# A macaron layer on one core: own phase plans for the first two and last two chunks, set-up in twelve steps, one more value and gate buffer

## The chip, the cores and the metric

The kernel runs on one core of a Trainium2 chip. The metric is the device time of one execution in microseconds (us). Three runs of the kernel before gave 1022.44, 1022.88 and 1028.41 us; the median is 1022.88 us.

## What is computed

The input x has 8 batches of 1024 positions with 256 channels. Three sublayers follow each other, each on a layer norm of its input:

```
x = x + 0.5 * ffn(layernorm(x))
x = x + attention(layernorm(x))
x = x + 0.5 * ffn(layernorm(x))
```

The feed-forward mixes each position with the one before it, and multiplies a sigmoid gate with a squared-ReLU network:

```
xr = mu_r * x + (1 - mu_r) * x_prev;  xk = mu_k * x + (1 - mu_k) * x_prev
ffn = sigmoid(xr @ W_r) * (square(relu(xk @ W_k)) @ W_v)
```

The attention has 16 heads of 16 channels. Each query looks at 40 fixed offsets back: 0 to 32, and 48, 64, 96, 128, 192, 256, 384. Its logit is `q.k * 0.25 * (1 + q.scale_embed[offset]) + pos_bias[offset]`; a softmax over the 40 logits weights the shifted values. The result is multiplied by a gain and by a sigmoid gate, and goes through an output projection.

## The kernel before

**Units of work.** A chunk is 256 positions; there are 32 (c = 0 to 31), four to a batch. A tile is 128 positions (tt = 0 to 63), two to a chunk. A pair is two chunks (i = 0 to 15). Each kind of work is a Python generator, whose `yield` cuts it into steps, and each step issues a few instructions:

- `f1`, `f2` (`ffn(c, "a")`, `ffn(c, "b")`): load of x (f1 only), statistics on DVE (L207), a chain of eight small POOL instructions for the normalisation (L212 to L219), normalised rows on ACT (L224) and their transposes on PE (L226), scaling on ACT (L241), the shifted part on DVE (L246), the products k, r and v on PE with relu, square and tanh on ACT (L263, L269, L271), the gated product on DVE (L278), the sum on POOL (L280), the output's DMA (L283, f2 only). f1 has 12 steps, f2 has 12.
- `p` (`project(c)`): statistics, normalisation and transposes as above, a split of the rows into two fp16 halves (L291, L292), the projections q, k, gate and value on PE (twelve fp16 matmuls each), `kst` on DVE (L317), `gt` on ACT (L329), the bias added to x on POOL (L341), `vn` on DVE (L343), and a DMA of the values to DRAM (L351).
- `far` (i, th) and `loc` (tt): the score products of far and near offsets on PE, copied out by ACT (L370) and written by DMA to DRAM (L397 and L411), from where a skewed read turns them into one row per query.
- `att` (`attend(tt)`), 18 steps: the skewed reads of the logits (`lg`, L425 and L429), reads of the shifted values (`vw`, `v3`, L435 to L445), the product `gp` with the scale embedding on PE, `lr` on DVE (L458), the bias on POOL (L461), maximum and subtraction on DVE (L464, L465), the exponential on ACT (L467) and, issued by ACT, the write of the probabilities to DRAM (L468), the far products on POOL (L482) and DVE (L489), the skewed read of the probabilities (`pd`, L497), the far sum on DVE (L505) and POOL (L508), eight transposes of pd on PE (L514) in two halves, each copied by ACT to `ptt` (L520), the value product `pv` on PE, division on DVE (L536 to L538), transposes (L547), the gate (L548), and for the chunk's second tile the output projection and the sum into x (L563). For a chunk's first tile the last step issues nothing.

All matmuls are issued by the helper `mm` (L195), so the profile gives them that line.

**The order.** There is no loop over chunks in which the work stands. Every step has a time: the place of its unit (c, tt/2 or 2i) plus an entry of the table `PLAN` for that kind and step, plus a shift of `WARP` for some kinds at chunks 0 to 3 and 22 to 31. All steps are sorted by these times and issued in this order, by hand (`tc.manual_schedule()`). The order counts per engine: each engine takes its instructions in the order in which they were issued, and waits for what the next one needs. DMAs of SP and ACT stand in their engines' queues in the same way. A unit of time is a chunk.

**Buffers.** `PVN = 5` buffers hold `vn` (read by the far products until two chunks later), `PGA = 4` hold the gate. Logits `lg` have four buffers, `pd` one, the transposes and pv share one PSUM bank, scores and gp have two banks for each half.

**Set-up** has three steps: the loads of weights; then zeros, and a scale, an fp16 cast and a remainder of the four attention weights as one block (L153 to L156); then the biases.

Of the kernel before, what the change touches and what calls it, by code (L numbers as in the profile page):

```python
# [12 lines left out]
ALU = mybir.AluOpType  # L13
# [6 lines left out]
NCH = B * N // 256  # L20
# [15 lines left out]
SF_T = 16 * ROW - 16  # L36
VPAD = 96
VROW = 2 * 8 * 17
PX1, PVN, PGA = 12, 5, 4
WS = 16.0  # L40
XN, LGB, PDB, PTB, YTB = 2, 4, 1, 2, 1

PLAN = {
    "setup": (94.301, 95.430, 96.861),
    "f1": (-6.891, -5.181, -4.113, -3.628, -3.556, -3.503, -3.223, -3.134, -3.030, -2.933, -2.814, -2.771),
    "p": (-2.636, -2.595, -2.382, -2.366, -2.209, -2.155, -2.084, -1.868, -1.644, -1.528, -1.432),
    "f2": (1.626, 1.748, 1.930, 2.004, 2.060, 2.208, 2.297, 2.414, 2.553, 2.580, 2.713, 4.437),
    "far": (  # L50
        (-0.987, -0.918),
        (-0.874, -0.608),
        (-0.990, -0.939),
        (-0.777, -0.772),
        (-0.751, -0.627),
        (-0.528, -0.523),
    ),
    "loc": (
        (-1.515, -1.348),
        (-0.848, -0.610),  # L60
        (-1.298, -1.048),
        (-1.496, -1.489),
    ),
    "att": (
        (-0.277, -0.025, -0.020, 0.011, 0.092, 0.296, 0.358, 0.413, 0.416, 0.471, 0.743, 0.779, 0.784, 0.838, 0.892, 0.971, 1.094, 13.222),
        (-0.404, 0.000, 0.016, 0.041, 0.111, 0.194, 0.295, 0.315, 0.427, 0.447, 0.621, 0.660, 0.673, 0.723, 0.824, 0.884, 0.938, 1.093),
    ),
}
WARP = {
    ("att", 0): 0.012, ("att", 1): 0.014, ("att", 2): 0.002, ("att", 3): -0.006, ("att", 22): 0.010, ("att", 23): 0.002, ("att", 24): -0.008, ("att", 25): 0.032, ("att", 26): 0.048, ("att", 27): 0.036, ("att", 28): 0.026, ("att", 29): -0.049, ("att", 30): -0.064, ("att", 31): -0.076,  # L70
    ("f1", 0): -1.203, ("f1", 1): -0.910, ("f1", 2): -0.739, ("f1", 3): 0.153, ("f1", 22): 0.006, ("f1", 23): 0.025, ("f1", 24): -0.009, ("f1", 25): -0.004, ("f1", 26): 0.009, ("f1", 27): 0.026, ("f1", 28): 0.017, ("f1", 29): 0.027, ("f1", 30): 0.045, ("f1", 31): 0.053,
    ("f2", 0): 0.006, ("f2", 1): 0.006, ("f2", 2): -0.013, ("f2", 3): 0.001, ("f2", 22): 0.006, ("f2", 23): -0.003, ("f2", 24): 0.043, ("f2", 25): 0.041, ("f2", 26): 0.025, ("f2", 27): 0.477, ("f2", 28): 0.422, ("f2", 29): 0.543, ("f2", 30): 0.373, ("f2", 31): 0.119,
    ("far", 0): -0.275, ("far", 2): -0.001, ("far", 22): 0.004, ("far", 24): 0.035, ("far", 26): 0.044, ("far", 28): 0.047, ("far", 30): -0.024,
    ("loc", 0): -0.699, ("loc", 1): -0.010, ("loc", 2): 0.023, ("loc", 3): 0.047, ("loc", 22): 0.037, ("loc", 23): 0.007, ("loc", 24): 0.043, ("loc", 25): 0.074, ("loc", 26): 0.045, ("loc", 27): 0.056, ("loc", 28): 0.007, ("loc", 29): 0.037, ("loc", 30): 0.014, ("loc", 31): 0.120,
    ("p", 0): -0.906, ("p", 1): -0.868, ("p", 2): -0.096, ("p", 3): 0.024, ("p", 22): -0.017, ("p", 23): -0.005, ("p", 24): 0.014, ("p", 25): 0.005, ("p", 26): -0.008, ("p", 27): -0.040, ("p", 28): 0.034, ("p", 29): 0.045, ("p", 30): 0.006, ("p", 31): -0.018,
}


# [5 lines left out]
def macaron(ctx: ExitStack, tc: tile.TileContext, x, wffn, watt, wo, cols, rows, pbias, se, mask, out):  # L84
    nc = tc.nc
# [14 lines left out]
    wa_hi = const.tile([128, 4, 2, 256], F16, name="wa_hi")  # L100
# [24 lines left out]
    def setup():  # L125
        with tc.tile_pool(name="setup", bufs=1) as sp:
            nc.sync.dma_start(w_f, wffn.rearrange("w (c p) d -> p w c d", p=128))
            wst = sp.tile([128, 4, 2, 256], F32, name="wst")
            nc.sync.dma_start(wst, watt.rearrange("w (c p) d -> p w c d", p=128))
            nc.sync.dma_start(row, rows.unsqueeze(0).to_broadcast([128, 2, 256]))  # L130
            zero = sp.tile([128, 4 * 512], F32, name="zero")
            nc.gpsimd.memset(zero, 0.0)
            nc.sync.dma_start(bias[:, 3].rearrange("p u e -> p (u e)"), pbias.to_broadcast([128, NO * 16]))
            msk = sp.tile([128, 3, NO], F32, name="msk")
            nc.sync.dma_start(msk, mask.rearrange("t p u -> p t u"))
            nc.sync.dma_start(wot, wo.rearrange("(c p) d -> p c d", p=128))
            se_f = sp.tile([128, NO], F32, name="se_f")
            nc.sync.dma_start(se_f, se.unsqueeze(0).to_broadcast([8, 16, NO]))
            yield
            nc.gpsimd.tensor_scalar(w_f[:, 2], w_f[:, 2], 0.25, 0.0, ALU.mult, ALU.add)  # L140
            for t in vw:
                nc.gpsimd.memset(t, 0.0)
            for t in ks:
                nc.gpsimd.memset(t[:, 0:LW], 0.0)
            for i in range(2):
                nc.sync.dma_start(v_d[i][0 : VPAD * VROW].rearrange("(p w) -> p w", p=VPAD), zero[:VPAD, :VROW])
            for sf in sf_d:
                nc.sync.dma_start(sf[0:PADF].rearrange("(p w) -> p w", p=16), zero[:16, : PADF // 16])
                for c0, c1, w in ((0, 5, 384), (5, 10, 384), (10, 15, 384), (15, 16, 368)):
                    o = PADF + c0 * ROW + ROW - 384  # L150
                    nc.sync.dma_start(flat(sf, o, (SF_T, 32), (ROW, c1 - c0), (1, w)), zero[:32, : (c1 - c0) * w])
            nc.sync.dma_start(flat(pd_d, NL * 16, (4 * SKEW, 128), (SKEW, 4), (1, SKEW - NL * 16)), zero[:, : 4 * 512])
            nc.vector.tensor_scalar(wst[:, 0], wst[:, 0], 0.25 * WS, None, ALU.mult)  # L153
            nc.vector.tensor_scalar(wst[:, 1:4], wst[:, 1:4], WS, None, ALU.mult)
            nc.scalar.copy(wa_hi, wst)
            nc.vector.tensor_tensor(wa_lo, wst, wa_hi, ALU.subtract)  # L156
            nc.vector.tensor_scalar(b_q, b_q, 0.25 * WS, None, ALU.mult)
            nc.vector.tensor_scalar(b_k, b_k, WS, None, ALU.mult)
            nc.vector.tensor_scalar(bv, bv, WS, None, ALU.mult)
            nc.vector.tensor_scalar(b_g, b_g, 0.5, None, ALU.mult)  # L160
            yield
            for t in range(3):
                nc.gpsimd.tensor_tensor(
                    bias[:, t], bias[:, 3], msk[:, t].unsqueeze(2).to_broadcast([128, NO, 16]), ALU.add
                )
            for c in range(2):
                nc.vector.tensor_scalar(wot[:, c], wot[:, c], gain[:, c : c + 1], 0.5 / WS, ALU.mult, ALU.mult)
            nc.vector.tensor_scalar(se_f, se_f, 4.0 / WS, None, ALU.mult)

            nc.vector.tensor_reduce(  # L170
                own.rearrange("p (h q) -> p h q", h=2),
                ident.rearrange("p (q h d) -> p h q d", q=4, h=2),
                AX.X,
                ALU.add,
            )
            nc.vector.tensor_reduce(
                kown.rearrange("p (h q) -> p h q", h=2),
                own.rearrange("p (h r q) -> p h q r", h=2, r=2),
                AX.X,
                ALU.add,  # L180
            )
            nc.vector.tensor_tensor(
                seb.rearrange("p u h q -> p u (h q)"),
                se_f.unsqueeze(2).to_broadcast([128, NO, 4]),
                kown.unsqueeze(1).to_broadcast([128, NO, 4]),
                ALU.mult,
            )
        lazy["pat"] = pool("pat", 2)
        lazy["pv1"] = pool("pv1", 2)
        yield  # L190
# [226 lines left out]
    def attend(tt):  # L417
# [149 lines left out]
    nc.vector.tensor_scalar(rest, col[:, 0:4], -1.0, 1.0, ALU.mult, ALU.add)  # L567
    steps = []
    move = lambda kind, place: place + WARP.get((kind, int(max(place, 0))), 0)
    add = lambda kind, place, gen, times: steps.extend(  # L570
        (move(kind, place) + t, kind, j, gen) for j, t in enumerate(times)
    )
    add("0", -100, setup(), PLAN["setup"])
    for c in range(NCH):
        add("f1", c, ffn(c, "a"), PLAN["f1"])
        add("p", c, project(c), PLAN["p"])
        add("f2", c, ffn(c, "b"), PLAN["f2"])
    for i in range(2 * B):
        for th in range(2 + 2 * (i % 2)):
            add("far", 2 * i, far(i, th), PLAN["far"][2 * (i % 2) + th])  # L580
    for tt in range(B * NT):
        add("loc", tt / 2, local(tt), PLAN["loc"][tt % 4])
        add("att", tt / 2, attend(tt), PLAN["att"][tt % 2])
    with tc.manual_schedule():
        for place, kind, j, gen in sorted(steps, key=lambda s: s[:3]):
            next(gen)
# [63 lines left out]
```

## Time and profile before

| | |
|---|---|
| median of three runs | 1022.88 us |
| the profiled execution: time, span | 1026.83 us, 1024.8 us |
| granted TensorE clock, mean | 0.971 |
| PE busy | 951.4 us (93%) |
| DVE, POOL, ACT busy | 831.9, 695.5, 610.4 us |
| DMA moved | 208.75 MB, 204 GB/s mean |

PE is TensorE's matmuls and PEld its weight loads, DVE the vector engine, ACT the scalar engine, POOL GpSimd, SP the engine that issues most DMAs. The ends of matmuls are modelled, so a busy PE is not one at its peak. A row such as "x<-y L224" is a group of instructions that write x from y at line 224. The chain that ended last is followed back from the last instruction; "issue" is time in which nothing shows that the engine waited for.

### The profile page before, as it was taken

What the parts mean: (1) busy time and instruction counts of PE and PEld (TensorE: products, weight loads), DVE (VectorE), ACT (ScalarE), POOL (GpSimd) and SP (SyncE); (2) the same over time, 40 slices, a digit from 0 to 9 for tenths busy, and PEclk for the clock granted to TensorE, in tenths of its full rate; (3) what the DMA queues carried; (4) which work ended last, traced back from release to release, by engine and by line L of the source; (5) the groups of instructions that cost most, each with busy time, mean ns of one, the idle gap of its engine ahead of it and who ended that gap; (6) DMA issues with size and microseconds to landing.
All of it is one profiled execution on the core that took longest, in us unless ns stands there. A gap on an engine that the chain in (4) does not pass through costs nothing.

```text
span 1024.8 us, 36078 instructions
## 1 busy us (share of the span) xinstructions
PE 951.4 (93%) x14592; PEld 781.3 (76%) x14592; DVE 831.9 (81%) x1670; ACT 610.4 (60%) x1218; POOL 695.5 (68%) x1240
## 2 busy tenths in 40 slices
PE   3888899999999999999999999999999999976775
PEld 2666688888888888888888888888888888854554
DVE  4446889988999789888999789988999789866761
ACT  3454666676666766676666766676666766543332
POOL 5434778767877688667787678767886778543641
PEclk9899999999999999999999999999999999988888
DMA  8257777768777776777877777688776777757530
GB/s 241 62 157 204 221 227 200 222 200 249 214 219 216 215 237 198 214 228 218 236 207 225 220 237 211 196 236 244 222 212 210 205 227 216 211 161 234 166 110 21
DMA packets 204365, 208.75 MB, mean 204 GB/s; under 512 B 77288, under 2 KB 162472, under 8 KB 204200
## 3 DMA queue, kind: packets, MB, share of 16 engines
q1 hardware_dynamic: 194984, 189.16, 64.8%
q10 hardware_dynamic: 9216, 17.31, 4.6%
q8 instruction: 114, 1.87, 0.8%
q14 instruction: 51, 0.42, 0.1%
HBM read 110.26 MB, written 96.14 MB: 201 GB/s over the span
## 4 chain that ended last, share of the span: by engine, by line
PE 81%; DMA 4%; POOL 4%; DVE 4%; issue 3%; ACT 2%; SPq 1%; ACTq 0%; POOLq 0%; DVEq 0%
PE p L195 55%; PE pv L195 6%; PE tra L195 5%; PE tra L514 5%; PE tr L226 5%; PE gp L195 4%; PE tra L547 1%; DMA lg<-sl 1%; ACT xn L224 1%; POOL y L213 1%; POOL x L280 1%; DMA sf<-sf 1%; DVE prod L505 1%; DMA pd<-pd 1%; DVE st L207 1%
## 5 line engine op out<-in xcount | busy, mean ns | idle before, releaser
L195 PE MATMUL p<-w_f,xm 128*128 128x256 f32 x1024 | 251.3, 389 | 0.0
L195 PEld LDWEIGHTS p<-w_f,xm 128*128 128x128 f32 x1024 | 187.5, 192 | 42.2 <-issue 12.7
L461 POOL TENSOR_TENSOR lg<-lg,bias 128x640 f32<-128x640 f32 x64 | 99.0, 1547 | 85.8 <-DVE lg L458 74.6
L195 PE MATMUL p<-xm,w_f 128*128 128x256 f32 x512 | 128.6, 396 | 8.4 <-DVE xm L248 5.2
L224 ACT ACTIVATE xn<-x,nb,y 128x256 f32<-128x256 f32 x192 | 104.9, 599 | 32.4 <-POOL nb L219 16.4
L241 ACT ACTIVATE xm<-tr,col 128x256 f32<-128x256 f32 x256 | 100.4, 475 | 39.8 <-PE tr L226 33.9
L195 PE MATMUL p<-kst,qst 64*32 64x256 f32 (+1 forms) x4096 | 123.6, 362 | 0.5 <-DVE kst L317 0.3
L246 DVE SCALAR_TENSOR_TENSOR xm<-tr,rest,xm 128x255 f32<-128x255 f32 x256 | 105.5, 474 | 21.2 <-ACT xm L241 19.9
L195 PEld LDWEIGHTS p<-xm,w_f 128*128 128x128 f32 x512 | 96.5, 198 | 25.6 <-issue 10.4
L508 POOL TENSOR_TENSOR far<-prod 128x272 f32<-128x272 f32 x64 | 49.0, 765 | 93.3 <-DVE prod L505 86.2
L280 POOL TENSOR_TENSOR x<-x,xm 128x512 f32<-128x512 f32 x64 | 81.9, 1279 | 39.9 <-DVE xm L278 39.9
L195 PE MATMUL p<-xh,wa_hi 128*128 128x256 f16 x384 | 105.1, 274 | 0.0
L195 PE MATMUL p<-xh,wa_lo 128*128 128x256 f16 x384 | 104.9, 273 | 0.0
L195 PE MATMUL p<-xl,wa_hi 128*128 128x256 f16 x384 | 104.9, 273 | 0.0
L482 POOL TENSOR_TENSOR prod<-vn,lg 128x272 f32<-128x272 f32 x144 | 94.9, 671 | 14.2 <-ACT lg L467 12.8
L520 ACT COPY ptt<-tra 128x512 f32<-128x512 f32 x128 | 74.7, 584 | 43.7 <-PE tra L514 27.8
L226 PE MATMUL tr<-ident,xn 128*128 128x128 f32 x384 | 66.4, 293 | 33.2 <-ACT xn L224 32.7
L505 DVE TENSOR_TENSOR prod<-prod 128x544 f32<-128x544 f32 (+2 forms) x120 | 93.6, 780 | 3.6
L195 PEld LDWEIGHTS pv<-vw,ptt 128*32 128x32 f32 x4096 | 69.2, 157 | 33.3 <-ACT ptt L520 17.3
L195 PEld LDWEIGHTS p<-kst,qst 64*32 64x32 f32 x4096 | 75.7, 122 | 22.9 <-issue 10.7
L317 DVE SCALAR_TENSOR_TENSOR kst<-p,col,kown 128x1024 f32<-128x1024 f32 x64 | 78.7, 1271 | 13.5 <-PE p L195 13.5
L514 PE MATMUL tra<-ident,pd 128*128 128x128 f32 x512 | 80.1, 280 | 10.3 <-DMA pd<-pd 6.7
(79 smaller groups left out, 2051.5 us busy)
## 6 DMA issues: line engine op xcount, KB each, us to landing
sl<-sl SPq DMA_DIRECT2D x256, 128.0 KB, 3.4
pd<-pd SPq DMA_DIRECT2D x64, 512.0 KB, 4.3
sf<-sf SPq DMA_DIRECT2D x184, 128.0 KB, 3.2
vw<-vd SPq DMA_DIRECT2D x128, 136.0 KB, 4.1
v<-vd SPq DMA_DIRECT2D x64, 272.0 KB, 4.4
lg<-sl SPq DMA_DIRECT2D x64, 264.0 KB, 3.9
pd<-lg ACTq DMA_DIRECT2D x64, 264.0 KB, 2.8
vd<-vn SPq DMA_DIRECT2D x32, 272.0 KB, 4.8
```

What stands on the lines that cost most here:

```text
L195: nc.tensor.matmul(o, l, r, start=start, stop=stop)
L224: nc.scalar.activation(xn, x2[:, i], AF.Identity, bias=nb[:, i : i + 1], scale=y[:, i : i + 1])
L226: nc.tensor.transpose(tr[:, c, i * 128 : i * 128 + 128], xn[:, c * 128 : c * 128 + 128], ident)
L241: nc.scalar.activation(xm[:, o, h], tr[:, h], AF.Identity, scale=mu[:, h : h + 1])
L246: nc.vector.scalar_tensor_tensor(x_[:, 1:256], tr[:, h, 0:255], m, x_[:, 1:256], ALU.mult, ALU.add)
L280: nc.gpsimd.tensor_tensor(x2, x2, xr, ALU.add)
L317: nc.vector.scalar_tensor_tensor(ks[g][:, o : o + 256], p[:, g].unsqueeze(2).to_broadcast([128, 256, 4]), b_k[:, g : g + 1], kown.unsqueez ...
L461: nc.gpsimd.tensor_tensor(la, la, bias[:, min(t, 3)].rearrange("p u e -> p (u e)"), ALU.add)
L482: nc.gpsimd.tensor_tensor(prod[:, k], shifted[k][1](), lf[:, k].unsqueeze(2).to_broadcast([128, 16, 17]), ALU.mult,)
L505: nc.vector.tensor_tensor(terms[:, 0:m], terms[:, 0:m], terms[:, n - m : n], ALU.add)
L514: nc.tensor.transpose(tr[:, pr * 128 : pr * 128 + 128], pd.rearrange("p (m e) -> p m e", e=8)[:, :, 4 * g + pr], ident,)
L520: nc.scalar.copy(ptt.rearrange("p q n -> p (q n)"), tr)
```

## The change

`PLAN` and `WARP` get new numbers throughout. Two further tables of the same form, `HEAD` and `TAIL`, give their own times to the units whose place is below 2 or at least 30. Set-up has twelve steps: loads; zeros; then for each of the four weights a scale with the cast, and the remainder; the small biases; the rest. `vn` gets a sixth buffer, the gate a fifth.

```
-PX1, PVN, PGA = 12, 5, 4
+PX1, PVN, PGA = 12, 6, 5
 PLAN = {
-    "setup": (94.301, 95.430, 96.861),
+    "setup": (94.361, 94.532, 95.582, 95.687, 95.775, 95.853, 96.126, 96.282, 96.369, 96.804, 96.866, 97.036),
...
+HEAD = {
+    "f1": (-6.555, -5.139, -4.717, -3.768, -3.673, -3.558, -3.147, -3.091, -2.947, -2.922, -2.780, -2.656),
+    "p": (-2.700, -2.641, -2.170, -2.154, -1.959, -1.928, -1.727, -1.604, -1.250, -1.218, -0.525),
+    "f2": (1.624, 1.726, 1.991, 2.003, 2.044, 2.194, 2.256, 2.425, 2.526, 2.582, 2.665, 4.550),
...
+TAIL = {
+    "f1": (-6.118, -4.991, -4.175, -3.572, -3.556, -3.482, -3.203, -3.104, -3.023, -2.888, -2.861, -2.805),
+    "p": (-2.647, -2.560, -2.392, -2.383, -2.187, -2.112, -2.095, -1.781, -1.576, -1.412, -1.106),
+    "f2": (1.501, 1.854, 2.001, 2.004, 2.155, 2.433, 2.502, 2.778, 2.976, 3.003, 3.284, 4.106),
...
+    "att": (
+        (-0.057, 0.016, 0.081, 0.107, 0.134, 0.268, 0.313, 0.436, 0.442, 0.487, 0.546, 0.744, 0.809, 0.847, 0.890, 1.001, 1.087, 12.895),
+        (-0.073, -0.052, 0.078, 0.098, 0.206, 0.277, 0.314, 0.347, 0.364, 0.438, 0.520, 0.524, 0.665, 0.769, 0.793, 0.879, 0.992, 1.151),
+    ),
+}
+ENDS = (2, 2)
...
-            nc.vector.tensor_scalar(wst[:, 0], wst[:, 0], 0.25 * WS, None, ALU.mult)
-            nc.vector.tensor_scalar(wst[:, 1:4], wst[:, 1:4], WS, None, ALU.mult)
-            nc.scalar.copy(wa_hi, wst)
-            nc.vector.tensor_tensor(wa_lo, wst, wa_hi, ALU.subtract)
+            yield
+            for w in range(4):
+                nc.vector.tensor_scalar(wst[:, w], wst[:, w], WS if w else 0.25 * WS, None, ALU.mult)
+                nc.scalar.copy(wa_hi[:, w], wst[:, w])
+                yield
+                nc.vector.tensor_tensor(wa_lo[:, w], wst[:, w], wa_hi[:, w], ALU.subtract)
+                yield
...
-    add = lambda kind, place, gen, times: steps.extend(
-        (move(kind, place) + t, kind, j, gen) for j, t in enumerate(times)
-    )
+    def add(kind, place, gen, n=0):
+        plan = HEAD if place < ENDS[0] else TAIL if place >= NCH - ENDS[1] else PLAN
+        times = PLAN["setup"] if kind == "0" else plan[kind] if kind in ("f1", "p", "f2") else plan[kind][n]
+        steps.extend((move(kind, place) + t, kind, j, gen) for j, t in enumerate(times))
```

What this does to the order, as sorting the old and the new times shows it: in chunks 4 to 21 each engine's list differs by a few exchanges of neighbours, and POOL takes f1's normalisation five places earlier. At the start, the local scores of tile 0 move from before to after the feed-forward of chunk 2; kst of chunk 0 moves behind the gated product of chunk 1. At the end, the second far-score group of the last pair moves ahead of the transposes of tile 57; the exponentials of tiles 58, 59 and 61 move ahead of ACT work that stood before them; the far sums on DVE move earlier by two to four places; the local-score writes of tiles 62 and 63 move on SP behind the read of tile 60's probabilities and ahead of the read of tile 61's; and from tile 63's value product on, all lists are as before.

## The prediction

> **What bounds the kernel now.** I read the page's first two parts, then busy time by stage, then the chain that ended last, then the timelines of single engines at both ends. The page says how large the whole is; the profiled execution took 1026.83 us, 2.0 more than its span and 3.95 more than the median of the three runs (1022.88). I count differences inside this execution and take them off the median.
>
> ```profile
> span 1024.8 us, 36078 instructions
> PE 951.4 (93%) x14592; PEld 781.3 (76%) x14592; DVE 831.9 (81%) x1670; ACT 610.4 (60%) x1218; POOL 695.5 (68%) x1240
> ```
>
> PE is idle for 73 us. The stages (columns: stage, its length, busy time of PE, PEld, DVE, ACT, POOL, granted clock, DMA share, GB/s) show where:
>
> ```profile
> 0.00:25.00 25.00, 9.34 (x32) 7.20 (x32) 12.15 (x34) 10.11 (x17) 12.55 (x34) 0.97 0.86 242
> 25.00:50.00 25.00, 19.87 (x141) 14.97 (x142) 11.25 (x30) 11.25 (x23) 12.56 (x28) 0.82 0.20 56
> 50.00:75.00 25.00, 21.52 (x347) 16.12 (x346) 12.47 (x26) 13.05 (x26) 7.65 (x26) 0.93 0.56 155
> 75.00:100.00 25.00, 20.99 (x288) 16.26 (x288) 16.27 (x30) 12.98 (x27) 13.06 (x24) 0.93 0.73 206
> ...
> 500.00:525.00 25.00, 25.00 (x489) 20.96 (x489) 23.71 (x48) 16.09 (x34) 20.66 (x36) 1.00 0.73 205
> ...
> 900.00:925.00 25.00, 19.01 (x343) 12.63 (x340) 15.82 (x30) 10.81 (x21) 10.43 (x16) 0.86 0.56 162
> 925.00:950.00 25.00, 15.53 (x275) 11.23 (x281) 13.01 (x25) 8.90 (x17) 11.66 (x18) 0.77 0.76 229
> 950.00:975.00 25.00, 18.38 (x282) 14.15 (x280) 19.55 (x36) 8.11 (x17) 15.95 (x24) 0.84 0.58 165
> 975.00:1000.00 25.00, 18.43 (x193) 14.31 (x193) 15.71 (x34) 8.52 (x18) 9.90 (x17) 0.84 0.33 106
> ```
>
> From 125 to 900 us the 31 stages leave 3.6 us of PE idle together: that stretch is PE's own work, and no order of the steps shortens it. The first 125 us hold 31 us of idle, the last 125 hold 39, at a granted clock of 0.77 to 0.86. So the change is worth what it does to two latency chains. The last one begins like this (start, length, what):
>
> ```profile
> 903.32 5.38 DMA pd<-pd
> 908.70 0.14 issue
> 908.83 1.09 PE tra L514 x4
> 909.92 3.60 PE p L195 x64
> ...
> 925.44 6.40 DMA sf<-sf
> 931.91 0.33 ACTq L468
> 932.24 0.05 issue
> 932.29 0.63 ACT xm L269
> 932.92 0.48 ACT ptt L520
> 933.44 1.22 PE pv L195 x60
> ```
>
> Tile 57 waits for its probabilities to come back from DRAM (pd); tile 58 waits because ACT stood from 927.5 to 931.9 at the DMA issue of tile 59's probabilities, which a far-score write (sf) released. I write pv57 for the value product of tile 57, f2-27 for the second feed-forward of chunk 27, and so on.
>
> **The middle.** I sorted the old and the new times of all steps and compared each engine's list. In chunk 15, PE's list differs by one exchange (a far score against the gate projection); DVE's by two, SP's by three places at most, POOL does the next feed-forward's normalisation five places earlier. PE has nothing to wait for there but rows that are early, so 0. Best case the 3.6 us go; worst, every one of some 24 chunks shows a wait like the smallest in PE's list of waits, 0.3 us for kst (L317): +7. Taken: 0.
>
> **The buffers.** vn of chunk c is read last by tile 2c+4 at c+2.41 and its buffer taken again, with five, at c+5-1.64 = c+3.36; gate is read last at c+1.44 and taken again, with four, at c+2.13. Both have 0.7 of a chunk (about 20 us) to spare, and no wait names them. The sixth and fifth buffer are worth 0; what hides this is that spare time. No instruction is added.
>
> **The head.** Set-up's scale, cast and remainder of four weights become twelve instructions instead of four. From rows of this trace: scales 4 x 0.43 (L153) against 0.43 + 0.94 is +0.35 on DVE; casts 4 x 0.59 (L291, same size) against 1.90 is +0.46 on ACT; remainders 4 x 0.69 (L292) against 2.29 is +0.47 on DVE. Both engines are under half busy in the first 25 us. On the path lies one scale, 0.43, ahead of the statistics of chunk 2 and then of chunk 0 (L207, 22.15): DVE is free at 20.8 + 0.43 + 1.2 = 22.4 instead of 22.15, +0.25. The normalised chunk 1 on ACT (18.77) now stands behind the third cast, which waits for that scale: it moves to 21.7, and its shift ends at 26.2 instead of 25.4. That hides behind PE's wait for chunk 0's normalisation until 27.75; without that cover it would cost 0.8. Then kst of chunk 0 (2.48 us, L317) goes behind chunk 1's L278 (37.21) and ahead of chunk 1's statistics, which start at 40.4 instead of 39.3; queued behind are POOL's normalisation (40.64) and PE's transposes (43.95): +1.1. Against it, the first local scores (1.96 us of PE at 45.06) move behind chunk 2's feed-forward, whose sum on POOL (57.43) comes 1.3 earlier. But chunk 1's bias sum (1.27, L341) now stands on POOL ahead of chunk 2's normalisation and eats that lead, so PE's transposes of chunk 2 stay at 64.8, the 0.25 and the 1.1 being inside these times, with 32 score matmuls (1.07, tile 1) left to do after them instead of before. Sum: 1.1 us late. Ends: -3.6 (one of the four gaps of 3.2 to 6.4 us closes) to +4.8 (one more such gap on top).
>
> **The tail**, by the durations above in the new order. (1) far score 1 of the last pair moves from behind tra57 into the wait ahead of it (1.1 of 5.5 us filled); tra57's halves now stand together, a copy of 0.59 between them (one PSUM bank), and far 2 and 3 run under the second copy: pv57 at 913.8 instead of 915.9. (2) ACT takes exp58 ahead of the evictions of far 2 and 3 (1.15 each): 912.2 instead of 915.1. Its write (5.5 us in the trace) and read (4.1) bring tra58 to 922.3 instead of 925.6. (3) far 3 is scored 5 us earlier, but its four DMA issues stand on SP behind the read of pd58 (918.5): landed about 924, not 931.8. Exp59's DMA is due at 925, so ACT no longer stands. What is late next is f2-27's shift on DVE, moved behind the far sum of tile 58: 927.2 instead of 923.3; PE holds f2-27's k for it with pv58 queued behind: pv58 at 929.2 instead of 933.4. (4) f2-27's v runs ahead of tra59, the far sum of tile 59 ahead of f2-28's statistics: pv59 at 938.5 (943.4), f2-28's transposes at 942 (948.3). Lead about 5. (5) On SP the read of pd61 now stands behind the local-score writes of tiles 62 and 63 (8 issues, 4.8 us) and lg62 (4 issues, 2.0): 958 instead of 960.9, where a lead of 5 would have given 956. (6) On DVE the far sum of tile 62 (1.76) moves ahead of lr63 (L458): it waits for POOL's products, 0.3 late. (7) pv63 at 987.4 instead of 991.9. After it every engine's list is as before: 1024.8 - 991.9 = 32.9 us, unchanged. Sum: -4.4. Ends: every step of the lead lost and (5) at its full 6.8 us late, +6.8; all three waits gone (5.5 + 4.0 + 3.8), -13.3.
>
> The four transposes after the 4.74 us wait took 1.09 us, those after a wait of 1.99 us at 965.83 took 0.69: a long wait also slows what follows. The Trainium skill's "TensorE: Matmul & The Clock Gate" (What's actually happening) says that the clock halves after an idle window of about 3.4 us and comes back after as long a busy one. By my walk 3.5 us of the first wait stay, just over that, so by the rule filling it buys no clock; were it under, the rule would make it some 0.7 us more (1.09 and 1.05 down to 0.69 each). I count none.
>
> **Forecast**: 1022.88 + 1.1 + 0 - 4.4 = 1019.6 us, chance 0.36.
>
> **Rivals.** *SP decides the tail, slower* (0.20): if lg62 has to wait until tile 63's scores have landed (SP did wait for sf landings at L429, 2.4 us once), the read of pd61 issues near 963 and lands at 967.7 instead of 965.8. It decides once that read issues after 960.9. For: writes of pd took 2.0 to 5.5 us to land and SP waits 30 us for them in this tail. Against: SP has pauses of 4 to 6 us. Price +1.9, with the head +1.1: 1025.9. *The waits close altogether* (0.22): the three tail waits (13.3) go, with the head's 1.1 against: 1010.7. For: they are waits for steps that this plan moves. Against: each has a DRAM round trip of 8 us in it. *No gain where it counts* (0.22): pd's round trip sets each tile's pace, a lead is given back at the next tile as in (5), and the head's loss hides: 1022.9.
>
> **How the numbers follow.** The likeliest gives 1019.6. Ends of the unknowns: best -3.6 - 3.6 - 13.3, worst 7 + 4.8 + 6.8; they won't all fall together, and 1009 to 1030 leaves out about 2 in 10. Within 1% (10.2 us, about what a measurement of this kernel can tell from no change): most of the likeliest, all of no gain, most of the SP rival, part of the closing waits, 0.63; faster by more, most of the closing waits and little else, 0.24; slower by more, the middle's and the head's bad ends with the SP rival, 0.13.
>
> **What would show it.** Right: PE saturated from 125 to 900 us with under 5 us idle; transposes of chunk 1's normalisation (L226) near 45; ACT without a stand at L468 near 927; pv58 four us earlier; about 33 us from pv63 to the end. Wrong: PE idle in the middle over 8 us, the L497 read of pd61 later than before, a head later by over 4 us, or a lead at pv58 that is gone at pv60.

## Result and the profile after

The changed kernel took 1029.65 us (median of 18 runs, 1026.34 to 1034.43); the kernel before, beside it, 1022.91 us (18 runs). The ratio is 1.0056 with an interval of [1.0035, 1.0077]: **slower by 5.7 us** (3.6 to 7.9), which is also the difference of the means; the medians lie 6.7 apart. The prediction was 1019.6 us, faster by 3.3. Below, 0.1% is 1.02 us.

The page of the kernel after, its first lines (compare 1024.8 us and PE 951.4 of before):

```profile
span 1029.3 us, 36062 instructions
PE 955.9 (93%) x14592; PEld 778.4 (76%) x14592; DVE 838.7 (81%) x1675; ACT 615.5 (60%) x1221; POOL 683.2 (66%) x1240
```

Busy time by stage of the kernel after, five of the stages that the prediction shows, with the same columns (stage, its length, busy time of PE, PEld, DVE, ACT, POOL, granted clock, DMA share, GB/s):

```profile
25.00:50.00 25.00, 17.29 (x94) 13.30 (x95) 16.25 (x37) 9.99 (x21) 12.33 (x29) 0.77 0.23 67
50.00:75.00 25.00, 21.04 (x317) 15.27 (x315) 8.31 (x18) 13.99 (x28) 8.76 (x27) 0.89 0.40 102
...
500.00:525.00 25.00, 25.00 (x486) 20.41 (x485) 23.71 (x49) 16.46 (x33) 19.55 (x36) 1.00 0.71 202
...
925.00:950.00 25.00, 18.34 (x310) 13.55 (x294) 16.45 (x30) 8.53 (x16) 9.59 (x14) 0.85 0.65 198
950.00:975.00 25.00, 16.97 (x216) 12.18 (x216) 19.90 (x34) 8.58 (x16) 15.68 (x19) 0.84 0.69 198
```

PE does 2.6 us less from 25 to 50 us (17.29 against 19.87), at a granted clock of 0.77 instead of 0.82. From 925 to 950 it does more than before (18.34 against 15.53), where PE of before waited 4.0 us behind ACT's stand at a DMA issue. The middle stage is as full as before: this view shows no loss there. Stages of fixed borders don't compare the same work, so I read both traces by their work: the end of the reciprocal in each tile's division (L537, after L588), counted in the order of the tiles. By it the profiled execution of after is 2.4 us late at tile 6, 3.5 at tile 44, 7.5 at tile 56, and 4.5 at the end. So in this pair of executions it loses in the middle, between tiles 44 and 56 most of all, and the tail wins back 3.0.

Now the chain of after in the tail (start, length, what), the place of the lines that the prediction showed. In the lines of after every line number from L195 on is 51 higher:

```profile
933.11 1.65 DVE xm L297 x4
934.76 0.10 DVE xm L299
...
934.90 3.78 PE p L246 x8
938.68 1.13 PE pv L246 x58
```

ACT's stand at the probabilities' DMA is gone from the chain. Instead the chain goes through the shift of f2-27 on DVE (933.11) and then through f2-27's k, eight matmuls in 3.78 us, with pv58 queued behind them.

### The profile page after: what moved, and what is told of

The parts are those of the page before. It is cut to its first block, busy times and chain, and to the rows that moved or that the text cites. A ratio compares the mean times of both kernels' runs of the same rounds, so it can differ in the third digit from the quotient of the medians.

```text
span 1029.3 us, 36062 instructions
## 1 busy us (share of the span) xinstructions
PE 955.9 (93%) x14592; PEld 778.4 (76%) x14592; DVE 838.7 (81%) x1675; ACT 615.5 (60%) x1221; POOL 683.2 (66%) x1240
## 3 DMA queue, kind: packets, MB, share of 16 engines
q1 hardware_dynamic: 194984, 189.16, 64.8%
## 4 chain that ended last, share of the span: by engine, by line
PE 78%; DMA 5%; DVE 4%; POOL 4%; issue 3%; SPq 3%; ACT 2%; ACTq 0%; POOLq 0%; DVEq 0%
PE p L246 53%; PE pv L246 7%; PE tra L565 5%; PE tra L246 5%; PE tr L277 4%; PE gp L246 4%; DMA pd<-pd 2%; DMA lg<-sl 2%; PE tra L598 1%; POOL y L264 1%; SPq L462 1%; POOL prod L533 1%; POOL lg L512 1%; DVE mx L515 1%; DVE prod L556 1%
## 5 line engine op out<-in xcount | busy, mean ns | idle before, releaser
L275 ACT ACTIVATE xn<-x,nb,y 128x256 f32<-128x256 f32 x192 | 104.8, 597 | 40.1 <-POOL nb L270 24.9
L533 POOL TENSOR_TENSOR prod<-vn,lg 128x272 f32<-128x272 f32 x144 | 108.5, 765 | 26.1 <-ACT lg L518 24.5
L556 DVE TENSOR_TENSOR prod<-prod 128x544 f32<-128x544 f32 (+2 forms) x120 | 96.9, 807 | 4.6 <-POOL prod L533 0.8
L246 PEld LDWEIGHTS pv<-vw,ptt 128*32 128x32 f32 x4096 | 69.2, 157 | 27.2 <-ACT ptt L571 8.9
L565 PEld LDWEIGHTS tra<-ident,pd 128*128 128x128 f32 x512 | 71.3, 190 | 22.8 <-ACT ptt L571 7.4
```

What stands on the lines that cost most here:

```text
L246: nc.tensor.matmul(o, l, r, start=start, stop=stop)
L275: nc.scalar.activation(xn, x2[:, i], AF.Identity, bias=nb[:, i : i + 1], scale=y[:, i : i + 1])
L533: nc.gpsimd.tensor_tensor(prod[:, k], shifted[k][1](), lf[:, k].unsqueeze(2).to_broadcast([128, 16, 17]), ALU.mult,)
L556: nc.vector.tensor_tensor(terms[:, 0:m], terms[:, 0:m], terms[:, n - m : n], ALU.add)
L565: nc.tensor.transpose(tr[:, pr * 128 : pr * 128 + 128], pd.rearrange("p (m e) -> p m e", e=8)[:, :, 4 * g + pr], ident,)
```

## Experiments

**Where does it lose? Cut by units.** A kernel takes the new times for some units and the old ones (`PLAN0`, `WARP0`) for the rest; e1 has the new set-up, e4 the added buffers:

```
+        new = place < 4        # e1; e2: 4 <= place < 27; e3: place >= 27; e4: place >= 4
+        plan = PLAN0 if not new else HEAD if place < ENDS[0] else TAIL if place >= NCH - ENDS[1] else PLAN
...
+        steps.extend((move(kind, place, new) + t, kind, j, gen) for j, t in enumerate(times))
```

> New set-up in twelve steps and new times for the units whose place is below 4; all other units keep the old times, and the buffers stay at five and four. Theory A, the loss is shared out as one pair of traces shows it (head +2, middle +4, tail -1.4): about 1025, +2. Theory B, the whole loss comes from the head and what drifts later is only its shadow or chance: about 1028.5, +5.8. The prediction's own step: +1.1.

> Old set-up, old times for units below 4 and from 27 on; new times for places 4 to 26 only. Theory A (many short waits of PE in the middle, hidden in a row that reads as busy): about 1026.5, +3.6. Theory B and the prediction: 1022.9, no change.

> New times for units from place 27 on, all else as before. Theory A: about 1021.5, -1.4, with tile 58's value product some 2 us earlier against the entry of the tail and the lead gone by tile 62. The prediction's step: -4.4. A third view, that the tail itself costs: +1 or more.

> All new (buffers six and five) except set-up and the units below 4, which are as before: the complement of the first run. Theory A: +2.2, about 1025. Theory B: 1022.9 or less, no change.

Measured: e1 1.0053 [1.0030, 1.0075], e2 1.0186 [1.0163, 1.0209], e3 1.0246 [1.0223, 1.0269], e4 1.0074 [1.0051, 1.0096]. The parts add up to far more than the whole. From tile 44 to tile 56, where e2 and e3 change plans at chunk 27, they took 182.7 and 196.9 us, where before took 169.2, and PE's busy time from 125 to 900 us is 762.3 and 758.1 us instead of 771.4: where one chunk on the old plan stands beside one on the new one, there are waits that neither plan has. These four cuts say little about the parts.

**Cut through the order instead.** All steps are sorted by the old times and by the new ones; the kernel issues the old list up to a time, then what is left by the new list, or the reverse:

```
+    take(old, 6.0)      # h4; h2: take(new, 6.0), take(old, 1e9); h3: take(old, 27.6), take(new, 1e9)
+    take(new, 27.6)
+    take(old, 1e9)
```

h1 is the old order with the added buffers (`PVN, PGA = 6, 5`); h2 has the new set-up and those buffers left at 5 and 4.

> The old order and the old set-up in every step; only the buffers are new (six value, five gate). Theory C, the buffers' addresses or their waits cost (the earlier pair that differs in them up to tile 6 stood at +3.4 and +7.1 there): +3, with the loss made before tile 6. All other theories: no change.

> The new order and set-up for every step due before 6.0 (about the first 190 us), then the remaining steps in the old order; buffers five and four. Cut through the order of steps and not through units, so that no unit is set against its neighbours. Theory A (shared loss): +2.4 at tile 6 and at the end. Theory B (all in the head): +5.8. The prediction's step: +1.1.

> The old order until 27.6 (about 875 us), the new one for all steps that are left; buffers five and four. Theory A: -1.4 at the end, with a lead of 2.4 at tile 58's division that is lost by tile 63. The prediction's step: -4.4, lead 4 to 5 at tile 58 and kept.

> The old order until 6.0, the new one until 27.6, then the old one; buffers five and four. Theory A: +3.5, gathered in small steps between tiles 6 and 55. Theory B and the prediction: 0 within a microsecond or two.

| kernel | new part | ratio | us |
|---|---|---|---|
| h1 | buffers | 0.9990 [0.9969, 1.0010] | -1.0 |
| h2 | head and set-up | 1.0013 [0.9988, 1.0037] | +1.3 |
| h4 | middle | 1.0042 [1.0015, 1.0070] | +4.3 |
| h3 | tail | 1.0006 [0.9983, 1.0029] | +0.6 |

Now the parts add up: 5.2 of 5.7 us. The middle alone is slower than no change; the tail's predicted -4.4 (0.9957) lies outside its interval.

**The middle: an engine's list, or a place?** The forecast named two kinds of exchange in the common chunks. m1 gives POOL its old order back in the new middle, m2 gives DVE its own:

```
-    "f1": (-6.939, -5.207, -4.426,      # m1
+    "f1": (-6.939, -5.207, -4.113,
...
-    "p": (-2.733, -2.582,               # m1: p's normalisation
+    "p": (-2.733, -2.595,
...
-    -2.375, ... -1.565                  # m2: p's split and its vn
+    -2.364, ... -1.528
```

> The new middle between 6.0 and 27.6 as before this, but POOL's order there is the old one: f1's normalisation five places later again, and p's normalisation ahead of an even tile's products. Theory M1 (POOL's order makes rows late, so that PE's transposes and products wait): the middle's +4.3 falls to about +1, PE's time in p's transposes and in the far scores (chunks 6 to 25) falls by 0.5 and 1.2 to the old sums. Theory M2 (it is DVE's order): +4.3 stays. Theory M3 (no single exchange): about +3.

> The new middle, but DVE's order there is the old one: statistics of f2 ahead of xl (L292 of the first kernel), the gate product of an odd tile ahead of vn. Theory M2 (DVE held by xl and vn, which wait for PE): the middle's +4.3 falls to about +1. Theory M1: stays at +4.3. Theory M3: about +3.

m1: 1.0051 [1.0020, 1.0081]. m2: 1.0041 [1.0017, 1.0065]. Neither list alone is the cause.

Then by place: m3 has the new order from 21.5 to 27.6 only, m4 from 6.0 to 21.5 only, and m5 has the new phases through the whole middle with the old `WARP` of chunks 22 to 26.

> The old order throughout, but for the steps whose time lies between 21.5 and 27.6, which follow the new order; old set-up and buffers. The new middle as a whole was 0.42% slower (+4.3 us). Theory A: the loss sits in the stretch where the chunks carry shifts of their own (chunk 22 and on), where every new order took 1.5 us longer from tile 44 to tile 50: then this kernel is slower by 2.5 to 4 us, ratio 1.0025 to 1.004. Theory B: the loss is a small toll of every chunk, some 0.2 us in each of 21: then it is slower by 1.2 us, ratio 1.001.

> The counterpart: the new order for the steps from 6.0 to 21.5 alone, where every chunk has the same plan, and the old one elsewhere. Theory A (the loss sits late): ratio 1.000 to 1.0015, at most 1.5 us. Theory B (a toll of every chunk): slower by about 3 us, ratio 1.003.

> The new order from 6.0 to 27.6 with the new phases, but with the old shifts of chunks 22 to 26; the old order elsewhere. If the new shifts of these chunks are what costs, ratio 1.000 to 1.0015; if the new phases cost it wherever they stand, ratio 1.003 to 1.0045, as the whole new middle.

m3: 0.9994 [0.9974, 1.0014]. m4: 1.0001 [0.9980, 1.0021]. Neither half alone shows a loss in its time, which fits neither theory: two halves at -0.5 us together against +4.3 for the whole. Each of these numbers is uncertain by 2 to 3 us. m5: 1.0187 [1.0151, 1.0224]: phases and shifts of different plans make seams again; it can't answer the question.

The traces can. Time from the division of tile 44 to that of tile 56:

| order there | executions | us |
|---|---|---|
| old | before, e1, h1, h2, h3, t1, t2, m4 | 169.2 to 170.9, mean 170.1 |
| new | after, e4, h4, m1, m2, m3, a1 | 171.9 to 173.2, mean 172.4 |

The two sets don't overlap: 2.3 us in 12 tiles. From tile 6 to tile 44 they do: 546.4 to 551.1 in the old order, 548.2 to 551.6 in the new one. In two places PE of the new order waits where PE of the old one doesn't: just ahead of the transposes of acc (L547) of tiles 49 and 51. In after the waits are 0.81 and 0.32 us; in the seven new executions 0.4 to 0.8 us at tile 49 and, but for m1, 0.3 to 0.4 us at tile 51; in the eight old ones none at either. Compared step by step with before, with the overlap of neighbouring matmuls that is lost there, they are 1.0 and 0.4 of the 2.3 us. First the group of all such transposes from 125 to 900 us (busy time, mean ns of one, idle time before them and what ended it). Before:

```profile
L547 PE MATMUL tra<-ident,acc 128*128 128x128 f32 x108 | 20.8, 274 | 0.0
```

After:

```profile
L598 PE MATMUL tra<-ident,acc 128*128 128x128 f32 x108 | 21.0, 276 | 1.3 <-DVE acc L589 1.3
```

And what stands between tile 49's value product and its transposes, in PE's timeline of before (start, length):

```profile
799.27 1.20 PE L195 MATMUL pv<-vw,ptt 128*32 128x34 f32 x64
...
801.61 0.27 PE L195 MATMUL p<-wa_hi,xl 128*128 128x256 f16 x1
801.72 0.60 PE L226 MATMUL tr<-ident,xn 128*128 128x128 f32 x4
802.16 0.38 PE L547 MATMUL tra<-ident,acc 128*128 128x128 f32 x2
```

In after (the view starts at 806 and so counts the last 34 of the 64 matmuls of the value product):

```profile
805.79 0.73 PE L246 MATMUL pv<-vw,ptt 128*32 128x34 f32 x34
806.45 0.66 PE L277 MATMUL tr<-ident,xn 128*128 128x128 f32 x4
807.92 0.41 PE L598 MATMUL tra<-ident,acc 128*128 128x128 f32 x2 [0.81 <-DVE acc L589]
```

On DVE in after, the division that PE waits for:

```profile
806.59 0.44 DVE L587 TENSOR_TENSOR far<-pv,far 128x272 f32<-128x272 f32 x1 [0.47 <-PE pv L246]
...
807.35 0.42 DVE L589 TENSOR_TENSOR acc<-far,rc 128x256 f32<-128x256 f32 x1
```

The division takes 1.2 us from the end of the value product. Before, the value projection of chunk 27 (twelve matmuls, 1.32 us) and four transposes cover it. In the new order the projection stands ahead of the value product, and the four transposes (0.44 us) alone can't. At tile 51 it is the transposes of chunk 30 that moved away. The tables show how close this was. In the old order the value product of tile 49 and the value projection of chunk 27 both stand at 25.316, and the product goes first; in the new one they stand at 25.284 and 25.260, above all because the shift of `p` at chunk 27 went from -0.040 to -0.088. At tile 51 the shift of `att` at chunk 25 went from 0.032 to -0.040, so that its transposes moved from 26.470 to 26.410, and those of chunk 30, ahead of them at 26.417, now stand behind them at 26.414. m6 is h4 with the cover back:

```
+    moved = {("p", 8, 27): 25.285, ("p", 9, 27): 25.370, ("f1", 3, 30): 26.405}
```

> The new middle as in h4, with three steps of the new order moved back to where the old order has them: the value projection of chunk 27 behind the value product of tile 49 instead of ahead of it, the write of its vn on DVE behind the division of tile 49, and the transposes of chunk 30's first normalisation ahead of the transposes of tile 51. Theory: the new middle loses there, because TensorE reaches the transposes of tiles 49 and 51 with too little work behind the value product and waits 1.0 and 0.4 us for DVE's division. Then the time from the division of tile 44 to that of tile 56 falls from 171.9 to 173.2 us, as every new order had it, to 169.5 to 171, as every old one had it; the transposes of chunk 29 end 0.44 us before those of tile 49 instead of 1.4; ratio 1.000 to 1.003 instead of 1.0042. Rival: the loss is a property of the new phases in all chunks; then the wait moves elsewhere, the stretch stays above 171.9 us and the ratio at 1.004.

m6: 1.0011 [0.9988, 1.0033], where h4 had 1.0042; the stretch 169.1 us, as in the old order. Tile 49 in its PE timeline:

```profile
807.57 0.60 PE L309 MATMUL tr<-ident,xn 128*128 128x128 f32 x4
808.09 0.41 PE L630 MATMUL tra<-ident,acc 128*128 128x128 f32 x2
```

The wait and the stretch's excess go together. The change of the time agrees (3.2 us), but the intervals of m6 and h4 overlap. And m3 is a warning: it shows both waits (0.82 and 0.30 us) and a stretch of 172.6 us, and its time, 0.9994, shows no loss. That these waits make the +4.3 us is not shown.

**The tail: what holds pv58?** h3 is the new tail alone. t1 moves f2-27's transposes, its scaling and its shift (steps 2 to 4 of f2) back to their old place ahead of the maximum of tile 59; its k keeps its new place behind the transposes of tile 58. t2 also puts tile 61's value loads, which wait for pv59, behind tile 60's read of pd and the score write of tile 62 on SP:

```
+    moved = {("f2", 2, 27): 29.4721, ("f2", 3, 27): 29.473, ("f2", 4, 27): 29.475}
+    moved.update({("att", 1, 61): 30.395, ("loc", 1, 62): 30.334, ("loc", 1, 63): 30.452})   # t2 only
```

> The new tail from 27.6 on, but the shift of f2 of chunk 27 on DVE (and its scaling on ACT) goes back to its old place ahead of chunk 28's projection sum and tile 59's maximum. Theory T (the lead is real up to tile 58's second copy and is lost on PE, which holds k of f2-27 for that shift with pv58 behind it): pv58's division 3 to 4 us earlier against tile 56's than in the new tail (30.7 becomes 27), and the rest of the tail 2 to 4 us shorter: 116 to 118 instead of 120. Rival (DVE's other work is only pushed back): no change, 120. In the median -2 to -4 against the new tail, so 0.996 to 0.998 of before.

> As the run before, and SP's order at tiles 60 to 62 nearly the old one: the read of pd60 ahead of tile 61's value loads, the local scores of tile 62 ahead of it, those of tile 63 right after. Theory T: tile 60's second copy another 2 us earlier, the tail 114 to 116 us, ratio about 0.995. Rival (pd's round trip sets the pace whatever SP does): as the run before.

t1: 0.9973 [0.9951, 0.9996], faster than before, if barely; h3's interval overlaps it. t2: 0.9975 [0.9950, 1.0000], the same as t1. In us after the division of tile 56, by execution:

| tail | write of tile 59's probabilities | f2-27's shift ends | its k takes | division of 58 | read of pd60 | end |
|---|---|---|---|---|---|---|
| old: before | 29.7 | 21.1 | 2.0 | 33.2 | 47.1 | 122.5 |
| old: e1, h1, h2, h4, m1 to m4, m6 | 25.3 to 27.2 | 20.0 to 21.8 | 1.8 | 28.8 to 30.8 | 42.4 to 45.5 | 115.1 to 121.6 |
| new: after, h3 | 22.9, 24.5 | 25.0, 25.1 | 3.7, 3.7 | 30.8, 30.9 | 46.3, 47.0 | 119.5, 120.5 |
| t1 | 22.6 | 18.5 | 3.4 | 27.2 | 43.7 | 115.8 |
| t2 | 22.5 | 18.4 | 3.0 | 27.0 | 39.8 | 114.8 |

Two more executions have the new order here, e3 and e4, but with seams ahead of it, and their tile 57 comes early (12.8 and 10.9 us after tile 56). Counted from the division of tile 57 to that of tile 58 they agree with the others: 16.7 to 16.8 us in after, h3, e3 and e4, against 13.3 to 14.3 with the shift back (t1, t2, and a1 and a2 below) and 13.0 to 15.0 in the nine old ones (17.3 in before).

Two readings. **First, the execution that the forecast read was an unlucky one.** Its ACT engine stood 4.4 us before the DMA issue of tile 59's probabilities; the nine other executions with the old tail stood 0.3 to 2.3 us. ACT's timeline of before (start, length, and in brackets the idle time ahead and what ended it):

```profile
931.91 0.33 ACTq L468 DMA_DIRECT2D pd<-lg  x1
932.29 0.63 ACT L269 ACTIVATE xm<-xm 128x512 f32<-128x512 f32 x1 [4.78 <-DMA sf<-sf]
```

The same place in h1, same order of steps:

```profile
932.15 0.33 ACTq L551 DMA_DIRECT2D pd<-lg  x1
932.52 0.63 ACT L352 ACTIVATE xm<-xm 128x512 f32<-128x512 f32 x1 [1.61 <-DMA sf<-sf]
```

What the forecast took off was mostly a chance of that execution. **Second, the new tail pays for its shift.** PE's timeline of h3 ahead of pv58:

```profile
921.81 0.71 PE L597 MATMUL tra<-ident,pd 128*128 128x128 f32 x4 [0.78 <-DVE x L646]
923.20 0.71 PE L597 MATMUL tra<-ident,pd 128*128 128x128 f32 x4 [0.68 <-ACT ptt L603]
926.86 3.78 PE L278 MATMUL p<-xm,w_f 128*128 128x256 f32 x8 [2.94 <-DVE xm L331]
930.57 1.19 PE L278 MATMUL pv<-vw,ptt 128*32 128x34 f32 x64
```

and of h1:

```profile
927.16 1.97 PE L278 MATMUL p<-xm,w_f 128*128 128x256 f32 x8 [0.44 <-DVE xm L331]
...
933.68 1.20 PE L278 MATMUL pv<-vw,ptt 128*32 128x34 f32 x64 [0.93 <-ACT ptt L603]
```

In h3, PE waits 2.94 us for the shift, and then takes 3.71 us (926.86 to 930.57) for a k that takes 1.80 in h1. The lead over the mean of the nine old ones, 1.6 us at tile 57, is lost at tile 58. t1, whose shift ends 6.5 us earlier, keeps it.

**Do the parts add up?** a1 is the whole change with t1's move, a2 with t1's and m6's. (The three steps that the next text calls scaling, shift and product k are t1's: transposes, scaling and shift.)

> The whole change, with three steps of the second feed-forward of chunk 27 (its scaling, its shift and its product k) moved back to where they stood before, as in t1. If the parts add up, the change's +5.8 us loses the 4.4 us that this took off the new tail (0.9973 against 1.0006, minus 3.3 us): ratio 1.002 to 1.0025. If another wait takes its place in the whole change, because the middle arrives later and in another state: ratio 1.0045 to 1.0055 as without the move.

> The whole change with both repairs: the three steps of the second feed-forward of chunk 27 back as in a1, and the cover of tiles 49 and 51 back as in m6. If the two stand for themselves, 1.4 us less than a1's 1.0014: ratio 0.9995 to 1.0005, the same as the kernel before, with the stretch from tile 44 to tile 56 at 169.5 to 171 us. If the middle's loss lies elsewhere: a1's 1.0014 or more.

a1: 1.0014 [0.9996, 1.0032], 4.3 us below the change's 1.0056, as the move gave h3 3.4. a2: 1.0022 [1.0002, 1.0042]: the further 1.4 us do not show. Its waits for the divisions of tiles 49 and 51 are gone (0.45 and 0.33 us in a1), but its stretch from tile 44 to 56 took 171.1 us, 0.85 less than a1's and 0.2 above the old orders' highest. By what was expected of it, this speaks for a loss of the middle that lies elsewhere, as far as intervals that overlap can say. The best version is t1 (t2 does the same): the old order with the new tail and its shift put back, 0.27% faster than the kernel before [0.04%, 0.49%].

## Why the prediction was wrong, step by step

**The middle, 0 (ends -3.6 to +7): the step that failed.** Measured +4.3 [+1.5, +7.2]. I compared the lists in chunk 15 and let it stand for all; the shifts of chunks 22 to 31 had changed too, and the loss that can be placed is there. Sorted in the same way, PE's list has 20 pairs of steps exchanged from 6.0 to 21.5, 1.3 a chunk, and 27 from 21.5 to 27.6, 4.4 a chunk. The reason given ("PE's own work, no order shortens it") says only that nothing can be won: an order can lengthen such a stretch by taking cover from one wait. The sign that I named, idle over 8 us, was no test either: from 125 to 900 us PE shows 4.0 us of idle after and 3.6 before, though two waits of 0.81 and 0.32 us are new. What is placed is 2.3 us from tile 44 to 56, and of that 1.4 at tiles 49 and 51. The cause of the +4.3 stays open beyond that: m3, which has these waits, and m4 show no loss in their times, and a2, which lacks them, is no faster than a1.

**The tail, -4.4: wrong twice.** Measured +0.6 [-1.7, +3.0]. Step (1) was right: tile 57's division came 14.0 us after tile 56's, where before, h1, h2 and h4 have 15.6 to 16.6. Step (3) was right that ACT hardly stands (0.03 us in after, 1.5 in h3) and that the shift is late next: it ended 25.0 us after tile 56's division, 24.9 by my walk. Its sizes failed: I allowed 2.0 us for f2-27's k, by the speed of the profiled execution, and it took 3.7, at half the granted clock, with waits ahead of it now. I had written that a long wait slows what follows, and did not apply it to the wait that I moved. So pv58 led the execution of before by 2.4 us instead of 4.2, and that execution's 4.4 us at L468 was no property of the old order. The rest of the lead went in steps (4) to (7): 1.4 us are left at tile 60's division and 0.3 at tile 62's, and pv63 began 89.5 us after tile 56's division, 89.6 in before, 85.1 by the walk. Step (5) had the read of pd61 at 55.7; it issued at 58.5, and at 58.6 before. Which wait took the lead there was not tested; a lead gone soon after pv58 was among the forecast's signs of being wrong. The last 32.9 us took 30.0; nine others with the old tail show 30.5 to 33.2, so part of this is scatter. The rival *no gain where it counts* describes the tail best. *SP decides* does not: t2 frees SP's read by 3.9 us against t1, and the time is the same.

The Trainium skill's "TensorE: Matmul & The Clock Gate" (What's actually happening) has the clock halve after an idle window of about 3.4 us. Here the longest single wait ahead of k was 2.94 us in h3 and 1.67 in t1, and k took 3.71 and 3.35 us instead of 1.80. The rows of k alone, with the columns of the stages (the granted clock is the third number from the right), of h3, h1 and a2:

```profile
926.86:930.57 3.71, 3.71 (x9) 2.52 (x9) 1.01 (x1) 0.19 (x1) 2.52 (x3) 0.50 0.31 111
927.16:928.96 1.80, 1.80 (x9) 1.59 (x9) 1.77 (x3) 0.80 (x2) 0.00 (x0) 1.00 0.96 201
929.56:931.42 1.86, 1.86 (x10) 1.34 (x9) 1.36 (x3) 1.33 (x2) 0.32 (x1) 1.00 1.17 341
```

So the clock was halved in h3 without a single wait of 3.4 us, and in t1 for most of k (0.54), with 0.7 us of transposes between shorter waits. But in a2 the same waits as in t1 (1.67 and 0.68 us) stand ahead of k, and the clock was full. The waits alone do not settle it, and what else does is not shown. For the forecast the rows decide: in its new place k took 3.0 to 3.7 us in seven of eight executions, 1.2 to 1.9 more than in the old one.

**The head, +1.1: consistent.** h2 measured +1.3 [-1.2, +3.8], which does not exclude 0. The chain of after shows the exchanges that were named:

```profile
38.68 2.39 DVE kst L368 x2
...
45.56 1.20 PE tr L277 x4
...
62.76 1.24 POOL x L392
```

One execution alone says little about the head: those with the old head and no seam reach tile 6 after 184.7 to 189.7 us, after, h2, a1 and a2 after 187.0 to 188.9. kst of chunk 0 now stands on the chain (between chunk 1's gated product, which ends at 38.7, and its statistics, from 41.07), the transposes come at 45.56 (walk: 43.95 + 1.1), and the bias sum (L392) stands on POOL ahead of chunk 2's normalisation, whose power (L264) starts at 64.36. That PE's transposes of chunk 2 "stay at 64.8" was too good: the group of eight there starts at 67.40, at 65.90 in h2.

**The buffers, 0: right** (h1, 0.9990). By the forecast's own numbers the spare time of `vn` is 0.95 of a chunk and not 0.7, which only helps. The range, 1009 to 1030, held the time in spite of the sign.

## What to carry to other kernels

A walk through a latency chain starts from one execution. A wait that is much longer than the same wait elsewhere may be a chance, and a gain read off it isn't one; an execution 4 us above its median says where to be careful. In a saturated stretch, an exchange of neighbours is judged by what it uncovers: look at each engine's round trip (product, division, transposes) and count the work between its two ends, in every chunk that has its own shift. And when an order is taken apart for a test, cut through the list of steps, not through the units: a seam between two plans cost 13 to 27 us here.

## What was not expected

- A step's time on PE jumps between executions of one order: f1's r products in chunks 6 to 21 took 29.2 to 29.6 us in four of six executions, 30.3 and 31.6 us in two. With the spread of the kernel before (1019.2 to 1031.7 us in 18 runs), 12 runs leave an uncertainty of 2 to 3 us.
- POOL's far products (128x272) took 765 ns each after, 671 before, though their code is the same. It goes with POOL's order: in m1, which has the old one, they took 684, in h4 731, and m1 was no faster than h4.
